# Moving the bias of an attention's softmax to ScalarE and fusing VectorE's three passes into one

## The chip, the cores and the metric

The kernel runs on one core of a Trainium2 chip. The metric is the device time of one execution in microseconds (us). The engines named here are TensorE (PE; its weight loads are shown apart, as PEld), VectorE (DVE), ScalarE (ACT), GpSimd (POOL) and SyncE (SP), which only issues transfers. Each engine takes its instructions strictly in the order of its own queue: an instruction that waits holds up all that stand behind it on that engine, and nothing else.

## The reference

A small transformer in float32 with T = 1024 tokens and C = 512 features: x = x + attention_a(LN(x)), then a feed-forward part, x = x + attention_b(LN(x)), and a second feed-forward part with the same weights. The change concerns attention_b alone, the second attention: 32 heads of 128 features in 8 groups of 4, one k and v per group, q and k normalised by the root of their mean square, and a bias that grows with the distance of two tokens.

```python
q = _rmsnorm(q, q_norm_w)
k = _rmsnorm(k, k_norm_w)
...
scores = jnp.einsum('bkgqd,bksd->bkgqs', qg, k) / math.sqrt(HD)
rel = pos[None, :] - pos[:, None]
bias = jnp.where(rel > 0, NEG_INF, slopes[:, :, None, None] * rel)
attn = jax.nn.softmax(scores + bias[None], axis=-1)
out = jnp.einsum('bkgqs,bksd->bkgqd', attn, v)
...
return out @ Wo.T
```

`rel` is never positive where a score counts (the mask is causal), and `slopes` has one number per head.

## The kernel before

Tokens are worked in 8 tiles of 128 (`NT`). For a query tile i only the keys of tiles 0 to i count, so a tile's row of scores is w = (i + 1) x 128 wide, 128 to 1024 columns, and is made in chunks of up to 512 columns (`QC`). The second attention is `attention_b`, L722 to L1151, some 475 to 1530 us of the profiled execution.

For each group g:

- `project_kv` (L810) makes k and v for 8 tiles on PE (L825). ACT sums k's squares (`ksq`, L833) and copies k and v out of PSUM (L835, L836); POOL scales k by its norm; k is transposed into `kT` (L862).
- `project_q` (L866) makes q for the 4 heads, each in two halves of 512 tokens (pq_h_0, pq_h_1; L878). The results lie in `ps_m`, a PSUM pool of two buffers. Of each half ACT writes the squares (`qsq`, L891), and after it VectorE the weighted q (`qT`, L893); then the buffer is free.
- `sum_squares` (L899) sums a head's squares on PE (st, L910), also in a buffer of `ps_m`; VectorE transposes the sums (`by`, L916), which frees the buffer, scales and shifts them (L920), and POOL raises them to the power -1/2 (`rsqrt`, L97, the instruction is L103). So `rq` holds, for each token, the reciprocal norm of q divided by the head's slope. It is needed by that head's softmax, later on.
- `softmax(g, hh, i)` (L923) does one tile of one head. PE makes the scores of a chunk (L932) into `ps_s`, again two buffers; VectorE writes p = s * rq + rel (L934), from PSUM into the tile's buffer p in SBUF. The mask lies in `rel` as a huge negative number. When the row is whole, VectorE takes its negated maximum (`nm`, L938) and multiplies it by the slope (L939); ACT computes exp(slope * p + nm) in place and sums the row (L941); VectorE takes the reciprocal (L943); POOL scales the row (L944). The pool `pp` has four buffers p (L760).
- `columns` (L957) turns p on VectorE in blocks of 32 x 32 (`pT` for the first four key tiles, L959; `tT` for the rest, L965). After the last of these p is free. `product` multiplies with v (L993), and ACT copies the result out (L1026).
- `project_o` (L737) multiplies with Wo (L742), and VectorE adds to x (L748).

A tile's `columns` come two tiles after its softmax (`LAG`, L1048). The main loop (L1087 to L1136) runs heads 0 to 3 of a group and tiles 7 down to 0. Between the softmaxes it spreads other matmuls as filler, so that PE has work while the softmax goes through VectorE and ACT: the next group's `project_kv`, then the output projection of the group before, then the next group's `project_q`. The shares are in `SHARE` (L1062). The last head of the last group runs its tiles upward.

The order of each engine's queue is decided by a scheduler when the kernel is built, from dependencies and priorities, so an edit in one place can move instructions elsewhere. A name such as s_3_6_0 is the score chunk of head 3, tile 6, from column 0; y_2 belongs to head 2. For odd tiles the rows are rotated by 32-row blocks, and `rels` holds `rel` and its rotated copy `relr`.

A fused pass of the kind that the change uses is there already: the first attention (L357) adds a mask to scores in PSUM and reduces them in the same instruction, with a constant scale and a mask in bf16.

Of the kernel before, what the change touches and what calls it, by code (L numbers as in the profile page):

```python
# [9 lines left out]
F32 = mybir.dt.float32  # L10
BF16 = mybir.dt.bfloat16
AF = mybir.ActivationFunctionType
ALU = mybir.AluOpType
AX = mybir.AxisListType
PSUM = bass.MemoryType.PSUM

P = 128
T = 1024
NT = T // P
# [6 lines left out]
NEG = -(2.0**100)  # L26
# [10 lines left out]
GRP = HB // HKV  # L37
DB = 128
B = 32
RMS_EPS = 1e-6  # L40
# [8 lines left out]
def alibi_slopes(n_heads):  # L49
    start = 2 ** (-(2 ** (-(math.log2(n_heads) - 3))))  # L50
    return [start * start**i for i in range(n_heads)]
# [13 lines left out]
class Block:  # L65
# [656 lines left out]
    def attention_b(self, ctx, wo_pool, WqT, WkT, WvT, WoT, qw, kw, xnT, missing, ffn_weights):  # L722
# [4 lines left out]
        nc, tc, sm = self.nc, self.tc, self.sm  # L727
        slopes = alibi_slopes(HB)
# [28 lines left out]
        with ExitStack() as ctx:  # L757
# [31 lines left out]
            rels = [self.rel, cp.tile([P, T], F32, tag="relr", name="relr")]  # L789
# [9 lines left out]
            kTs, vs, qTs, rqs = {}, {}, {}, {}  # L799
# [50 lines left out]
            def by_tile(t, i0, i1, turn=-1):  # L850


                v = t[:, i0 * P : i1 * P].rearrange("p (i a c) -> p a i c", a=P // B, c=B)
                return v[:, :, i0 % 2 :: 2], v[:, ::turn, 1 - i0 % 2 :: 2]
# [3 lines left out]
            def k_columns(g, half, k_sb, kT):  # L858

                pool, tag = (ps_m, "m") if g else (ps_s, "s")  # L860
                ps = self.transpose4(pool, [k_sb[:, a, :] for a in range(4)], f"k{g}{half}", tag=tag)
                nc.scalar.activation(  # L862
                    kT[:, half * QC : (half + 1) * QC], ps.rearrange("p a b -> p (a b)"), AF.Copy, scale=kw_sb
                )

            def project_q(g, wq):  # L866

                qTs[g] = []
                rqs[g] = []
                for hh in range(GRP):  # L870
                    qT = qp.tile([P, T], F32, tag="qT", name=f"qT{g}_{hh}")
                    qTs[g].append(qT)
                    rqs[g].append(sm.tile([P, NT], F32, tag="rq", name=f"rq{g}_{hh}", bufs=6))
                    for qc in range(NQC):
                        cols = slice(qc * QC, (qc + 1) * QC)
                        ps = ps_m.tile([P, QC], F32, tag="m", name=f"pq{g}_{hh}_{qc}")
                        for kc in range(KC):
                            nc.tensor.matmul(  # L878
                                ps, lhsT=wq[:, kc, hh * DB : (hh + 1) * DB], rhs=xnT[:, kc, cols], start=(kc == 0), stop=(kc == KC - 1)
                            )  # L880
                            if kc < KC - 1:
                                yield
                            if kc == 2 and qc == 0 and squares:

                                sum_squares(*squares.pop(0))
                            if kc == 1 and g and later:
                                k_columns(*later.pop(0))
                        if qc == 0:
                            sq = work.tile([P, T], F32, tag="w", name=f"qsq{g}_{hh}", bufs=1)
                        for to, of in zip(by_tile(sq, qc * 4, qc * 4 + 4), by_tile(ps, 0, 4, 1)):  # L890
                            nc.scalar.activation(to, of, AF.Square)  # L891
                        for to, of in zip(by_tile(qT, qc * 4, qc * 4 + 4), by_tile(ps, 0, 4, 1)):
                            nc.vector.tensor_scalar_mul(to, of, qw_sb)  # L893
                        yield
                        if later and not g:
                            k_columns(*later.pop(0))
                    squares.append((g, hh, sq))

            def sum_squares(g, hh, sq_T, behind=False):  # L899

                rq = rqs[g][hh]
                st = ps_m.tile([P, QC], F32, tag="m", name=f"st{g}_{hh}")[:, : NT * B]
                for a, sq in enumerate(sq_T.rearrange("p (i a c) -> a p i c", a=P // B, c=B)):
                    with ExitStack() as ctx:
                        if behind:
                            ctx.enter_context(tc.high_priority(offset=2000))
                        ins = nc.tensor.matmul(  # L910
                            st[a * B : (a + 1) * B, :].rearrange("p (i c) -> p i c", c=B), lhsT=ones, rhs=sq, start=True, stop=True
                        )
                        if behind:
                            tc.keep_in_program_order(ins)
                by_token = work.tile([P, NT, B], F32, tag="st", name=f"by{g}_{hh}", bufs=1)
                nc.vector.transpose(by_token.rearrange("p i c -> p (i c)"), st)  # L916


                s2 = slopes[g * GRP + hh] ** 2
                nc.vector.tensor_scalar(rq, by_token[:, :, 0], s2, DB * RMS_EPS * s2, ALU.mult, ALU.add)  # L920
                self.rsqrt(rq, rq, [NT])

            def softmax(g, hh, i):  # L923
                slope = slopes[g * GRP + hh]
                qT, kT, rq = qTs[g][hh], kTs[g], rqs[g][hh]
                w = (i + 1) * P
                n = f"{g}_{hh}_{i}"
                p = pp.tile([P, T], F32, tag="p", name=f"p{n}")
                for lo in range(0, w, QC):
                    hi = min(lo + QC, w)  # L930
                    s = ps_s.tile([P, QC], F32, tag="s", name=f"s{n}_{lo}")[:, : hi - lo]
                    nc.tensor.matmul(s, lhsT=qT[:, i * P : (i + 1) * P], rhs=kT[:, lo:hi], start=True, stop=True)  # L932
                    at = (NT - 1 - i) * P
                    nc.vector.scalar_tensor_tensor(  # L934
                        p[:, lo:hi], s, rq[:, i : i + 1], rels[i % 2][:, at + lo : at + hi], ALU.mult, ALU.add
                    )
                nm = sm.tile([P, 1], F32, tag="nm", name=f"nm{n}")
                nc.vector.tensor_reduce(nm, p[:, :w], AX.X, ALU.max, negate=True)  # L938
                nc.vector.tensor_scalar_mul(nm, nm, slope)  # L939
                ss = sm.tile([P, 1], F32, tag="ss", name=f"ss{n}")  # L940
                nc.scalar.activation(p[:, :w], p[:, :w], AF.Exp, bias=nm, scale=slope, accum_out=ss)  # L941
                rs = sm.tile([P, 1], F32, tag="rs", name=f"rs{n}")
                nc.vector.reciprocal(rs, ss)  # L943
                nc.gpsimd.tensor_scalar(p[:, :w], p[:, :w], rs, 1.0, ALU.mult, ALU.mult)  # L944
                return p
# [104 lines left out]
            for n, _ in enumerate(in_turn(project_kv(0, wkv), project_q(0, wq))):  # L1050
                missing(n, ps_s, "s")
# [12 lines left out]
            def finish(g, hh, i, p):  # L1064
                while rest:
                    product_rest(*rest.pop(0))
                columns(hh, p, i)
                last = g == HKV - 1
                if last and hh == GRP - 1:

                    if i == NT // 2 - 1:
                        product(g, hh, 0, NT // 2)
                    elif i == NT - 1:
                        product(g, hh, NT // 2, NT, whole=True)
                elif i == 0:
                    product(g, hh, 0, NT, whole=last and hh > 1)
                    while squares:
                        sum_squares(*squares.pop(0), behind=True)
                    if hh == GRP - 1:
                        while kept:  # L1080
                            copies(*kept.pop(0))
                    if last and hh == 1:
                        product_rest(g, heads[:2])
                    elif not last and hh == GRP - 1:
                        rest.append((g, heads))

            for g in range(HKV):  # L1087
# [4 lines left out]
                if not last:  # L1092
                    wq, wkv = load_qkv(g + 1)
                    parts.append(project_kv(g + 1, wkv))
                    parts.append(project_q(g + 1, wq))
# [8 lines left out]
                for hh in range(GRP):  # L1104
# [8 lines left out]
                    for at, i in enumerate(range(NT) if last and hh == GRP - 1 else down):  # L1113
                        p = softmax(g, hh, i)
                        n = hh * NT + at + 1
# [189 lines left out]
```

## Time and profile before

| what | value |
|---|---|
| median of 3 runs | 1589.62 us (1589.33 to 1589.82) |
| profiled execution, span | 1587.1 us |
| PE busy | 1576.2 us |
| DVE busy | 1084.9 us |
| ACT busy | 569.7 us |
| POOL busy | 364.4 us |
| granted PE clock | 1.00 throughout |

The profiled execution's own time is known by its span, 1587.1 us, from its first to its last instruction; the median of the runs lies 2.5 us above it. A group line of the profile reads: line of the code, engine, operation, output <- inputs, shapes and count, then the busy time of all and the mean duration of one in ns, then the time that the engine was idle just before them and what ended it. A line of waits reads: engine and instruction, what it waited for, us in total, how many times, the longest. A line of a timeline reads: start in us, duration in us, engine, line, operation, output <- inputs, count of records. A float32 matmul leaves two records.

### The profile page before, as it was taken

The numbers are of one execution on the slowest core, as the hardware profiler recorded it, in microseconds if no ns is written. First come the engines' busy times: TensorE is split into PE (matmuls) and PEld (weight loads), VectorE is DVE, ScalarE is ACT, GpSimd is POOL, SyncE is SP. The second block draws the span as 40 slices with busy tenths as digits, with TensorE's granted clock in tenths as the row PEclk, the third lists the DMA queues.
The fourth block names the chain that finished last, engine by engine and source line by source line (L and its number), as shares of the span: only waits on it lengthen the run. The fifth ranks groups of instructions, "written<-read, shape, count | busy, mean of one in ns | idle before, by whom it ended". The sixth has DMA issues, their size and how long they took to land.

```text
span 1587.1 us, 31573 instructions
## 1 busy us (share of the span) xinstructions
PE 1576.2 (99%) x12574; PEld 934.3 (59%) x12574; DVE 1084.9 (68%) x2841; ACT 569.7 (36%) x1397; POOL 364.4 (23%) x480
## 2 busy tenths in 40 slices
PE   9999999999999999999999999999999999999999
PEld 5545555555566557657556655756665566566654
DVE  4558788773535895775786678587667757777753
ACT  2216666664223443233233223323423322322330
POOL 3000000002222333222223213222322222222350
PEclk9999999999999999999999999999999999999999
DMA  5000332222022002002100200200110020010001
GB/s 206 1 1 6 24 20 18 20 19 63 1 72 70 20 27 68 27 1 55 40 27 28 68 27 1 73 22 28 45 49 27 27 74 28 1 54 28 2 2 53
DMA packets 66419, 56.42 MB, mean 36 GB/s; under 512 B 9504, under 2 KB 51232, under 8 KB 66272
## 3 DMA queue, kind: packets, MB, share of 16 engines
q1 hardware_dynamic: 64960, 50.46, 13.7%
q0 software_dynamic: 784, 2.90, 0.5%
q8 instruction: 99, 1.62, 0.4%
q10 hardware_dynamic: 528, 1.05, 0.2%
q14 instruction: 48, 0.39, 0.1%
HBM read 30.98 MB, written 2.10 MB: 21 GB/s over the span
## 4 chain that ended last, share of the span: by engine, by line
PE 95%; DVE 2%; POOL 1%; ACT 1%; issue 0%; DVEq 0%; ACTq 0%; POOLq 0%
PE s L932 15%; PE pq L878 14%; PE wo L742 13%; PE o L993 11%; PE sT L386 8%; PE kv L825 6%; PE oT L428 5%; PE or L993 4%; PE pm_f L693 3%; PE s L337 3%; PE pj_v L197 2%; PE pj_q L197 2%; PE pm_ao L1185 2%; PE pj_k L197 2%; PE st L910 1%; PE sT L406 1%
## 5 line engine op out<-in xcount | busy, mean ns | idle before, releaser
L941 ACT ACTIVATE p<-p,nm 128x1024 f32<-128x1024 f32 (+7 forms) x256 | 198.1, 774 | 379.9 <-DVE nm L939 362.0
L944 POOL TENSOR_SCALAR p<-p,rs 128x1024 f32<-128x1024 f32 (+7 forms) x256 | 191.0, 748 | 583.7 <-DVE rs L943 563.8
L932 PE MATMUL s<-kT,qT 128*128 128x512 f32 (+3 forms) x768 | 294.7, 492 | 0.7 <-DVE p L934 0.5
L878 PE MATMUL pq<-xnTb,wq 128*128 128x512 f32 x512 | 241.0, 596 | 0.0
L932 PEld LDWEIGHTS s<-kT,qT 128*128 128x128 f32 x768 | 141.4, 190 | 168.8 <-issue 111.4
L742 PE MATMUL wo<-wo,oT 128*128 128x512 f32 x512 | 239.7, 593 | 0.8 <-ACT spare L750 0.8
L959 DVE STREAM_TRANSPOSE pT<-p 128x512 f32<-128x512 f32 (+3 forms) x256 | 152.9, 603 | 80.3 <-PE o L993 47.4
L938 DVE TENSOR_REDUCE nm<-p 128x1 f32<-128x1024 f32 (+7 forms) x256 | 188.0, 735 | 2.8
L993 PEld LDWEIGHTS o<-pT,va 32*128 32x128 f32 x4212 | 174.4, 185 | 22.4 <-issue 11.5
L408 ACT ACTIVATE p<-sT 128x512 f32<-128x512 f32 (+1 forms) x292 | 155.2, 592 | 90.0 <-PE s L337 35.1
L993 PE MATMUL o<-pT,va 32*128 32x224 f32 (+5 forms) x4212 | 181.3, 324 | 0.0
L337 PE MATMUL s<-kT,qT 32*128 32x512 f32 (+3 forms) x768 | 164.5, 520 | 0.0
L386 PE MATMUL sT<-qT,kT 32*128 32x128 f32 (+3 forms) x1152 | 155.5, 402 | 0.4 <-ACT p L408 0.4
L742 PEld LDWEIGHTS wo<-wo,oT 128*128 128x128 f32 x512 | 94.7, 190 | 89.2 <-issue 77.2
L878 PEld LDWEIGHTS pq<-xnTb,wq 128*128 128x128 f32 x512 | 92.9, 190 | 90.0 <-issue 77.9
L934 DVE SCALAR_TENSOR_TENSOR p<-s,rq,relr 128x512 f32<-128x512 f32 x192 | 121.0, 644 | 11.3 <-PE s L932 11.2
L825 PE MATMUL kv<-wkv,xnTb 128*128 128x256 f32 x512 | 118.2, 381 | 0.2
L965 DVE STREAM_TRANSPOSE tT<-p 128x512 f32<-128x512 f32 (+3 forms) x128 | 63.9, 499 | 74.8 <-PE or L993 45.9
L934 DVE SCALAR_TENSOR_TENSOR p<-s,rq,rel 128x512 f32<-128x512 f32 (+1 forms) x192 | 103.5, 560 | 11.9 <-PE s L932 10.9
L386 PEld LDWEIGHTS sT<-qT,kT 32*128 32x128 f32 x1152 | 80.7, 184 | 50.7 <-issue 28.6
L825 PEld LDWEIGHTS kv<-wkv,xnTb 128*128 128x128 f32 x512 | 95.1, 190 | 20.9 <-issue 3.4
L354 DVE TENSOR_REDUCE part<-s 128x1 f32<-128x512 f32 x128 | 81.5, 684 | 28.2 <-PE s L337 20.1
(156 smaller groups left out, 1716.6 us busy)
## 6 DMA issues: line engine op xcount, KB each, us to landing
va<-v SPq DMA_DIRECT2D x256, 64.0 KB
wq<-in_b_WqT_dram SPq DMA_DIRECT2D x8, 1024.0 KB
wo<-in_b_WoT_dram SPq DMA_DIRECT2D x8, 1024.0 KB
x<-in_x_dram SPq DMA_DIRECT2D x8, 256.0 KB
wkv<-in_b_WkT_dram SPq DMA_DIRECT2D x8, 256.0 KB
wkv<-in_b_WvT_dram SPq DMA_DIRECT2D x8, 256.0 KB
out_dram<-x SPq DMA_DIRECT2D x7, 256.0 KB
o<-oTs SPq DMA_DIRECT2D x48, 32.0 KB
```

What stands on the lines that cost most here:

```text
L337: nc.tensor.matmul(made[j][:, at:end], lhsT=qT[rows_of(j), c, i * P : (i + 1) * P], rhs=kT[rows_of(j), c, kc * QC : kc * QC + end - at], s ...
L386: nc.tensor.matmul(made[j][:, at:end], lhsT=kT[rows_of(j), c, b * P : (b + 1) * P], rhs=qT[rows_of(j), c, qc * QC + x0 : qc * QC + x1], st ...
L408: nc.scalar.activation(p[:, j, :end], made[j][:, :end], AF.Exp)
L742: nc.tensor.matmul(ps, lhsT=oTs[g, h][:, t * P : (t + 1) * P], rhs=wo[:, h, :], start=(h == heads[0]), stop=(h == heads[-1]))
L825: nc.tensor.matmul(ps.rearrange("p a b -> p (a b)"), lhsT=xnT[:, kc, i * P : (i + 1) * P], rhs=wkv[:, kc].rearrange("p a b -> p (a b)"), s ...
L878: nc.tensor.matmul(ps, lhsT=wq[:, kc, hh * DB : (hh + 1) * DB], rhs=xnT[:, kc, cols], start=(kc == 0), stop=(kc == KC - 1))
L932: nc.tensor.matmul(s, lhsT=qT[:, i * P : (i + 1) * P], rhs=kT[:, lo:hi], start=True, stop=True)
L934: nc.vector.scalar_tensor_tensor(p[:, lo:hi], s, rq[:, i : i + 1], rels[i % 2][:, at + lo : at + hi], ALU.mult, ALU.add)
L938: nc.vector.tensor_reduce(nm, p[:, :w], AX.X, ALU.max, negate=True)
L941: nc.scalar.activation(p[:, :w], p[:, :w], AF.Exp, bias=nm, scale=slope, accum_out=ss)
L944: nc.gpsimd.tensor_scalar(p[:, :w], p[:, :w], rs, 1.0, ALU.mult, ALU.mult)
L993: nc.tensor.matmul(cols(o[:, a], j, j + skip), lhsT=vs[g][j // 4][rows, j % 4 * NB + b, :], rhs=moving(j, j + skip, rows, slice(b * B, (b ...
```

## The change

With y = (sum of squares) + 128 eps, the old kernel keeps rq = 1 / (slope * sqrt(y)) and computes s * rq + rel, of which softmax takes slope times. The new one keeps -1 / sqrt(y) in `rq`, and a second column `irq` = slope * sqrt(y), made on VectorE as y * slope * y^(-1/2). Now

- ACT writes rel * irq (128 x w, one factor per row) into the tile's buffer p before the scores come (new activation with Copy);
- VectorE adds the scores to it, multiplies by -1 / sqrt(y) and takes the running minimum, in one `tensor_tensor_reduce` per chunk; the minimum of the first chunk is the start of the second;
- ACT's Exp takes this minimum as its bias and -1 as its scale.

The separate reduce and the multiplication of its result by the slope are gone. In `sum_squares` VectorE has two more small instructions per head: `irq`, which reads POOL's power, and the negation of `rq`. The pool for `rq` gets a second tag for `irq`; `nm` has 6 buffers. Nothing changes on PE, POOL and the transfers but the order in which the scheduler puts a few of them.

```diff
-                    rqs[g].append(sm.tile([P, NT], F32, tag="rq", name=f"rq{g}_{hh}", bufs=6))
+                    rqs[g].append([sm.tile([P, NT], F32, tag=t, name=f"{t}{g}_{hh}", bufs=6) for t in ("rq", "irq")])
...
-                s2 = slopes[g * GRP + hh] ** 2
-                nc.vector.tensor_scalar(rq, by_token[:, :, 0], s2, DB * RMS_EPS * s2, ALU.mult, ALU.add)
-                self.rsqrt(rq, rq, [NT])
+                y = sm.tile([P, NT], F32, tag="y", name=f"y{g}_{hh}")
+                nc.vector.tensor_scalar_add(y, by_token[:, :, 0], DB * RMS_EPS)
+                self.rsqrt(rq, y, [NT])
+
+                nc.vector.scalar_tensor_tensor(irq, y, slopes[g * GRP + hh], rq, ALU.mult, ALU.mult)
+                nc.vector.tensor_scalar_mul(rq, rq, -1.0)
...
+                at = (NT - 1 - i) * P
+
+                nc.scalar.activation(p[:, :w], rels[i % 2][:, at : at + w], AF.Copy, scale=irq[:, i : i + 1])
+                nm = -NEG
                 for lo in range(0, w, QC):
...
-                    at = (NT - 1 - i) * P
-                    nc.vector.scalar_tensor_tensor(
-                        p[:, lo:hi], s, rq[:, i : i + 1], rels[i % 2][:, at + lo : at + hi], ALU.mult, ALU.add
-                    )
-                nm = sm.tile([P, 1], F32, tag="nm", name=f"nm{n}")
-                nc.vector.tensor_reduce(nm, p[:, :w], AX.X, ALU.max, negate=True)
-                nc.vector.tensor_scalar_mul(nm, nm, slope)
+                    least = sm.tile([P, 1], F32, tag="nm", name=f"nm{n}_{lo}", bufs=6)
+                    nc.vector.tensor_tensor_reduce(
+                        out=p[:, lo:hi],
+                        in0=s,
+                        in1=p[:, lo:hi],
+                        scale=rq[:, i : i + 1],
+                        scalar=nm,
+                        op0=ALU.add,
+                        op1=ALU.min,
+                        accum_out=least,
+                    )
+                    nm = least
                 ss = sm.tile([P, 1], F32, tag="ss", name=f"ss{n}")
-                nc.scalar.activation(p[:, :w], p[:, :w], AF.Exp, bias=nm, scale=slope, accum_out=ss)
+                nc.scalar.activation(p[:, :w], p[:, :w], AF.Exp, bias=nm, scale=-1.0, accum_out=ss)
```

In the changed kernel the new instructions are at L920 (y), L921 (power), L923 (irq), L924 (negation), L933 (bias copy), L940 (fused pass) and L952 (Exp).

More of the change, by code (lines that the diff above doesn't have):

```diff
@@ L899, in sum_squares @@
             def sum_squares(g, hh, sq_T, behind=False):
-                rq = rqs[g][hh]
+                rq, irq = rqs[g][hh]
                 st = ps_m.tile([P, QC], F32, tag="m", name=f"st{g}_{hh}")[:, : NT * B]
@@ L916, in sum_squares @@
                 nc.vector.transpose(by_token.rearrange("p i c -> p (i c)"), st)
-                s2 = slopes[g * GRP + hh] ** 2
-                nc.vector.tensor_scalar(rq, by_token[:, :, 0], s2, DB * RMS_EPS * s2, ALU.mult, ALU.add)
-                self.rsqrt(rq, rq, [NT])
+                y = sm.tile([P, NT], F32, tag="y", name=f"y{g}_{hh}")
[3 more added lines that the diff above has]
+                nc.vector.tensor_scalar_mul(rq, rq, -1.0)
             def softmax(g, hh, i):
-                slope = slopes[g * GRP + hh]
-                qT, kT, rq = qTs[g][hh], kTs[g], rqs[g][hh]
+                qT, kT, (rq, irq) = qTs[g][hh], kTs[g], rqs[g][hh]
                 w = (i + 1) * P
```

## The prediction

> **What bounds the kernel now.** I read first the page's busy shares and its chain of work, then stretches of the second attention one by one, then the groups of instructions by form, then the waits, and last the timeline of one place.
>
> ```profile
> span 1587.1 us, 31573 instructions
> PE 1576.2 (99%) x12574; PEld 934.3 (59%) x12574; DVE 1084.9 (68%) x2841; ACT 569.7 (36%) x1397; POOL 364.4 (23%) x480
> ...
> PE 95%; DVE 2%; POOL 1%; ACT 1%; issue 0%; DVEq 0%; ACTq 0%; POOLq 0%
> ```
>
> TensorE (PE) is the bound: 95% of the chain. A busy share is an average, so here are two stretches of the second attention (about 475 to 1530 us), and the sum over 500 to 1500 us. The columns are PE, PEld, DVE, ACT and POOL busy, then the granted clock.
>
> ```profile
> 600.00:700.00 100.00, 99.97 (x724) 60.77 (x720) 71.01 (x173) 29.23 (x78) 25.12 (x36) 1.00 0.14 38
> 900.00:1000.00 100.00, 100.00 (x632) 56.91 (x631) 78.79 (x195) 33.40 (x87) 25.35 (x31) 1.00 0.09 29
> sum 1000.00, PE 999.22 PEld 615.96 DVE 733.81 ACT 328.37 POOL 273.88; mean PE 99.92 PEld 61.60 DVE 73.38 ACT 32.84 POOL 27.39
> ```
>
> In the whole stage PE is idle for 0.8 us, at a clock of 1.00. Busy time can hide slack, so I also compared starts: a record of 512 columns is followed by the next after 429 ns where nothing disturbs, 384 after 322, 256 after 215. From 490 to 1500 us all matmuls together start only 15 us later than this, 122 times by about 104 ns. So work taken off VectorE (DVE) can bring little, while a wait that reaches PE costs its full length. The question is what the change does to in-order queues, not to sums.
>
> The rows that price the change (line, engine, operation, count | busy us, mean ns | idle before):
>
> ```profile
> L938 DVE TENSOR_REDUCE nm<-p 128x1 f32<-128x1024 f32 (+7 forms) x256 | 188.0, 735 | 2.8
> ...
> L939 DVE TENSOR_SCALAR nm<-nm 128x1 f32<-128x1 f32 x256 | 35.3, 138 | 2.6
> L357 DVE CUSTOM_DVE_ANT_0 junk<-s,mask,part 128x512 f32<-128x512 f32 x32 | 22.1, 729 | 6.4 <-PE s L337 6.4
> L357 DVE DVE_READ_ACCUMULATOR2_ANT neg<- 128x1 f32 x256 | 21.0, 82 | 0.0
> ...
> L941 ACT ACTIVATE p<-p,nm 128x1024 f32<-128x1024 f32 (+7 forms) x256 | 198.1, 774 | 379.9 <-DVE nm L939 362.0
> ...
> L103 POOL TENSOR_TENSOR rq<-rq,mhalf 128x8 f32<-128x8 f32 x32 | 52.6, 1645 | 90.7 <-DVE rq L920 90.0
> ```
>
> The last one matters most: the power of -1/2 on GpSimd (POOL) takes 1645 ns. Before, no VectorE instruction waits for it except, much later, the scores of that head.
>
> **The change part by part.**
>
> *Removed from DVE*: 256 reduces, 188.0 us, and 256 small scalings, 35.3 us.
>
> *Replaced on DVE*: 384 scalar-tensor-tensor passes (L934, 730 to 738 ns at 512 columns, 224.5 us in all) become 384 fused passes, each of two instructions. Its nearest row is the first attention's fused pass, the same call with a PSUM source: 729 ns at 512 columns, and 82 ns for reading the accumulator; its second source is bf16, here f32. From below 688 + 82 (the row without a running scalar); from above 730 + 672, the old pass and the 512-column reduce. I take 729 + 82 as the closest row: about +31 us for 384. Together DVE loses some 180 us (with the additions below), 68% to 57% of the span. Hidden under PE either way: worth nothing by itself.
>
> [...]
>
> *Added on ACT*: 256 bias copies (128 x w, a scale per row). Priced by the Exp rows without their accumulator read, 198.1 us (128 columns 399, 1024 columns 1148); from below by 186 (the scaled copy into kT takes 688 at 512 columns where Exp takes 721), from above by 198.1 + 48.1, if a read as after each Exp came along. ACT goes from 36% to 48%. By load it is hidden; but ACT's queue is in order, and Exps and the squares of q (`qsq`, L891) now stand behind copies that wait for a free buffer among four, or for `irq`.
>
> *Added on DVE, 32 times*: `irq` (0.2 us, priced by L920's 201) and the negation (0.15, by L939), 11 us. `irq` waits for the POOL power. In the changed kernel's order it stands right behind y or one chunk later, so DVE stands about 1.6 us at it, 32 times. Behind it wait fused passes (which free the two score buffers), the q evictions `qT` and the transposes `by` (which free the two buffers of `ps_m`). PE waits for those. Price: from below nothing, where PE holds enough queued work; from above 1.65 us x 32 = 53 us by itself.
>
> *The order.* Some other DVE instructions move too. The place I work out is the end of head 2's q projection, before it (matmul, then VectorE):
>
> ```profile
> 851.55 0.64 PE L910 MATMUL st<-qsq,ones 128*32 128x256 f32 x8
> 852.12 1.98 PE L878 MATMUL pq<-xnTb,wq 128*128 128x512 f32 x4
> ```
>
> ```profile
> 849.18 0.85 DVE L893 TENSOR_SCALAR qT<-pq,qw_sb 128x256 f32<-128x256 f32 x2
> ...
> 852.26 0.45 DVE L916 STREAM_TRANSPOSE by<-st 128x256 f32<-128x256 f32 x1
> ...
> 853.57 0.71 DVE L959 STREAM_TRANSPOSE pT<-p 128x512 f32<-128x512 f32 x1
> ```
>
> The sums st are done at 852.12, `by` frees their buffer by 852.71, and pq_3_1 (head 3, second half), which needs that buffer, is due at 852.98. In the changed order `by` stands behind the transposes pT of tiles 4 and 3 of the running head and the pass of tile 2; pq_3_1 is due at 852.98 + 0.43 = 853.41, as scores of 256 columns come first. The chain by rows, with 0.05 to 0.1 us per handover: the sums before end 839.75, their `by` (431), pT of tile 6 (701) and y_1 (201) 841.1; power to 842.85; irq_1 843.05; second pass of tile 5 (480 + 82) 843.65; its Exp (931 + 188) 844.85, on ACT ahead of qsq (2 halves, 0.66) 845.5; qT 846.4; pass of tile 4, 847.2; pT of tile 5 (0.70) 847.9; second chunk of tile 4 (346 + 82, overlapped) 848.25; its Exp (826 + 188) 849.3; qsq 849.95; qT 850.85; pass of tile 3 (811) 851.65; pT and tT of tile 4, 852.55; meanwhile Exp of tile 3 (721 + 188) 852.6; reciprocal 852.8; POOL (695) 853.55; pT of tile 3, 854.3; pass of tile 2 (613 + 82) 855.0; `by` (431) 855.4. That is 2.0 us after pq_3_1 is due; with the delays carried into it I had 2.25.
>
> In the same way, for one group: pq_1_1 waits 1.7 us for `by` of head 0 (behind the pass of tile 1, pT of tile 2 and their POOL multiply); the first scores of tile 6 of head 3 wait 0.6, of tile 3 0.25, of the next head's tile 7 0.1; kv_1 of the next group waits 0.6 for qT of pq_3_1 (now behind the last pT; before, qT ends 860.45 and kv_1 starts in time at 860.61); kv_2 0.35 for ACT. Heads 0 and 1, where the filler is the output projection and no irq falls, keep 0.35 to 0.7 us of slack: nothing. Sum 5.85 per group, six full preparations: 35; the first group some 4; the start of the stage 1.4 (ACT's four first copies, 3.9 us, wait for irq_0 ahead of qsq of pq_1_1, so the next sums' buffer comes late): 40.
>
> Places under 0.5 us are below what such chains resolve, and the first group was worked out least. I take the four larger: 1.7 + 0.6 + 2.25 + 0.6 = 5.15, x 6 = 30.9, + 1.4 = 32 us. Nothing is deducted for the tail (at 1511 to 1516 us PE waits 1.0 us for ACT and 0.8 us for a transpose), since ACT is busier there and DVE less.
>
> The profiled execution's span is 1587.1; the median of the runs is 1589.62, 2.5 us more, taken as unchanged. Forecast 1589.6 + 32 = about 1621 us, +2.0%.
>
> **The rivals.**
>
> *Hidden (1589, within 0.2%).* For it: DVE and ACT keep over 40% idle, each tile loses a reduce (0.28 to 1.20 us) and a scaling before its Exp, which shortens the chain as much as irq lengthens it, and sums and `by` are seldom urgent. Against it: before, `by` meets its deadline at the place above by 0.27 us only. Its price is 0 to 3 us.
>
> *Faster (about 1585).* 40 of the 104-ns delays lie between two score matmuls; if all are late passes on DVE and go, 4.2 us, with 1 us of the tail. More than the 15 us of all excess starts can't be had in this stage, so 1575 is the floor. Against it: the same delays occur between q-projection matmuls of one buffer, where DVE has no part. It decides only if the irq waits never reach PE.
>
> *Slower by far (about 1655).* The fused pass costs its upper bound, 730 + 672 at 512 columns, 0.59 us more than I took. The passes cover 32 heads x 4608 = 147,456 columns, so 170 us come back to DVE; DVE is then as busy as before but with longer single steps, and each maximum is up to 1.2 us later. If a fifth of it reaches PE, as through the same buffers, 34 us come on top of the 32. It decides from about 1.0 us per pass, where the fused pass costs more than the row of the reduce gave back. For it: 362 us of ACT's idle time are waits for nm, so every Exp follows its maximum closely. Against it: the row with a PSUM source and a running scalar shows no such cost.
>
> **How the numbers follow.** A measurement of this kernel tells about 0.2% from no change. Slower as worked out (1595 to 1640): 0.60; slower by far: 0.16; hidden: 0.13; faster: 0.09; the rest, 0.02, is a gain beyond the tail's. Slower by over 0.2% is 0.60 + 0.16 and a part of hidden, 0.77; same 0.13 less that part, 0.12; faster 0.11. The range goes down to 1587, leaving out faster, and up to 1655, leaving out half of slower by far. The likeliest case's own range is from one place per group at its bare slack (1.2 us x 6, 1597) to all 40 us and a quarter more, 1640.
>
> **What would show it.** Right: DVE waits for POOL at irq, some 30 times, 40 us or more; PE waits in the preparing stretches (pq for `by`, scores for the pass, kv for qT), none while the output projection fills; DVE near 905 us, ACT near 768, clock 1.00. Wrong: PE still above 99.5% in 500 to 1500 us (hidden); the fused pass far from 811 at 512 columns with its read; waits of PE spread evenly over all heads (ACT as a second clock).

## The result and the profile after

The changed kernel takes 1616.75 us (median of 4 runs, 1615.92 to 1616.95) against 1589.57 us: ratio 1.017, 95% interval 1.0155 to 1.0184. The profiled execution's span is 1615.0 us, 27.9 us above that of before. The page of the changed kernel, its span, busy shares, chain and two of its groups:

```profile
span 1615.0 us, 32171 instructions
...
PE 1585.9 (98%) x12574; PEld 931.5 (58%) x12574; DVE 917.6 (57%) x2777; ACT 744.8 (46%) x1653; POOL 364.8 (23%) x480
...
PE 75%; DVE 11%; POOL 6%; ACT 4%; issue 3%; SPq 1%; DMA 0%; POOLq 0%; DVEq 0%; ACTq 0%
...
L938 PE MATMUL s<-kT,qT 128*128 128x512 f32 (+3 forms) x768 | 296.9, 495 | 6.5 <-DVE nm L940 6.4
...
L878 PE MATMUL pq<-xnTb,wq 128*128 128x512 f32 x512 | 242.9, 599 | 8.1 <-DVE by L916 8.1
```

VectorE lost 167 us of work, ScalarE gained 175, and PE, which does the same 12574 matmuls at the same clock, 1.00, now stands: the chain runs through PE for 75% of the span instead of 95%. Most of the rest, 21%, goes through the loop VectorE, POOL, ScalarE. The idle time in the last column is what PE waits, and for whom.

Busy time by stretch, the same two as before and the sum over 500 to 1500 us (columns PE, PEld, DVE, ACT, POOL):

```profile
600.00:700.00 100.00, 99.23 (x733) 62.16 (x732) 52.23 (x156) 45.10 (x109) 24.70 (x35) 1.00 0.14 38
900.00:1000.00 100.00, 98.95 (x620) 54.62 (x620) 60.97 (x182) 48.48 (x102) 25.12 (x33) 1.00 0.09 27
sum 1000.00, PE 985.20 PEld 598.41 DVE 557.87 ACT 484.71 POOL 262.80; mean PE 98.52 PEld 59.84 DVE 55.79 ACT 48.47 POOL 26.28
```

PE stands 14.8 us in these 1000 us, where it stood 0.8, and of the other engines none is above 56% in the sum. No engine took PE's place as the bound; PE waits for the length of chains.

Comparing the starts of successive matmuls with the dense spacing, as in the prediction, accounts for the whole difference. The table sums how much later than this spacing the matmuls start, its excess, from 470 us on, in us:

| kernel | up to group 2's k and v | six groups | last group and after | sum |
|---|---|---|---|---|
| before | 3.0 | 10.4 | 7.0 | 20.5 |
| changed | 7.8 | 29.7 | 11.4 | 48.9 |

The sums differ by 28.4, the spans by 27.9. The six groups (1 to 6, in which the k, v and q of groups 2 to 7 are made) lose 3.2 us each, two thirds of it at the same three places each time: 0.94 us ahead of pq_1_1, 0.74 ahead of pq_3_1 and 0.45 ahead of the first scores of head 3's tile 6. The remainder, about 1.1 us a group, comes in small pieces: 0.15 to 0.2 us at k and v (0.5 to 0.6 at kv_1 in two of the groups), partly there before, and more of the 104-ns delays.

What PE waits for between 600 and 1420 us, by the view of waits (us in total, times, longest):

```profile
PE pq L878 <- DVE by L916: 8.1, 12, 0.8
PE s L938 <- DVE nm L940: 2.0, 7, 0.3
PE kv L825 <- DVE qT L893: 0.3, 1, 0.3
```

Twelve waits for `by`, two for each of six groups. And VectorE's new wait, from the same view over the whole run:

```profile
DVE irq L923 <- POOL rq L103: 44.2, 32, 1.8
```

The place that the prediction worked out in group 2, here at the end of group 1 of the changed kernel (timeline, VectorE, then PE):

```profile
724.84 0.71 DVE L970 STREAM_TRANSPOSE pT<-p 128x512 f32<-128x512 f32 x1 [0.89 <-POOL p L955]
725.48 0.58 DVE L940 CUSTOM_DVE_ANT_0 p<-s,p,rq 128x384 f32<-128x384 f32 x1
...
725.98 0.45 DVE L916 STREAM_TRANSPOSE by<-st 128x256 f32<-128x256 f32 x1
...
728.39 0.17 DVE L923 SCALAR_TENSOR_TENSOR irq<-y,rq 128x8 f32<-128x8 f32 x1 [1.76 <-POOL rq L103]
```

```profile
723.77 0.64 PE L910 MATMUL st<-qsq,ones 128*32 128x256 f32 x8
...
726.48 1.98 PE L878 MATMUL pq<-xnTb,wq 128*128 128x512 f32 x4 [0.58 <-DVE by L916]
```

The sums are done at about 724.4. `by` could start then, but ahead of it in VectorE's queue stands pT of tile 3, which waits 0.89 us for POOL's multiply, and then the pass of tile 2. So `by` ends at 726.43 and pq_3_1 starts at 726.48. The irq wait of 1.76 us comes after `by` and isn't itself ahead of pq_3_1; the one of the head before, 13 us earlier, is in the chain: without it, in the first run below, this place doesn't wait.

### The profile page after: what moved, and what is told of

Read it like the earlier page. It is cut to its first block, busy times and chain, and to the rows that moved or that the text cites. A ratio compares the mean times of both kernels' runs of the same rounds, so it can differ in the third digit from the quotient of the medians.

```text
span 1615.0 us, 32171 instructions
## 1 busy us (share of the span) xinstructions
PE 1585.9 (98%) x12574; PEld 931.5 (58%) x12574; DVE 917.6 (57%) x2777; ACT 744.8 (46%) x1653; POOL 364.8 (23%) x480
## 4 chain that ended last, share of the span: by engine, by line
PE 75%; DVE 11%; POOL 6%; ACT 4%; issue 3%; SPq 1%; DMA 0%; POOLq 0%; DVEq 0%; ACTq 0%
PE o L1004 12%; PE wo L742 11%; PE s L938 9%; PE sT L386 8%; PE kv L825 6%; PE oT L428 5%; DVE p L940 4%; PE pm_f L693 3%; PE or L1004 3%; DVE pT L970 3%; PE pq L878 3%; PE s L337 3%; POOL p L955 2%; ACT p L952 2%; POOL rq L103 2%
## 5 line engine op out<-in xcount | busy, mean ns | idle before, releaser
L952 ACT ACTIVATE p<-p,nm 128x1024 f32<-128x1024 f32 (+7 forms) x256 | 197.1, 770 | 210.7 <-DVE nm L940 197.2
L940 DVE CUSTOM_DVE_ANT_0 p<-s,p,rq 128x512 f32<-128x512 f32 (+3 forms) x256 | 159.9, 626 | 17.8 <-PE s L938 16.9
L933 ACT ACTIVATE p<-relr,irq 128x1024 f32<-128x1024 f32 (+3 forms) x128 | 106.1, 829 | 115.1 <-DVE tT L976 67.7
L933 ACT ACTIVATE p<-rel,irq 128x896 f32<-128x896 f32 (+3 forms) x128 | 92.0, 719 | 50.8 <-DVE pT L970 28.2
L954 DVE RECIPROCAL rs<-ss 128x1 f32<-128x1 f32 x256 | 40.3, 157 | 124.1 <-ACT p L952 123.2
```

What stands on the lines that cost most here:

```text
L933: nc.scalar.activation(p[:, :w], rels[i % 2][:, at : at + w], AF.Copy, scale=irq[:, i : i + 1])
L940: nc.vector.tensor_tensor_reduce(out=p[:, lo:hi], in0=s, in1=p[:, lo:hi], scale=rq[:, i : i + 1], scalar=nm, op0=ALU.add, op1=ALU.min, acc ...
```

## The experiments

Three causes were possible, and the prediction had mixed them: (1) VectorE stands at irq; (2) `by` stands behind transposes that wait for Exp, reciprocal and POOL, an order that comes with the shorter fused pass; (3) the bias copies hold up ScalarE's queue. The first four runs take away or add one at a time.

**irq on POOL**, so that VectorE never waits for the power:

```diff
-                nc.vector.scalar_tensor_tensor(irq, y, slopes[g * GRP + hh], rq, ALU.mult, ALU.mult)
-                nc.vector.tensor_scalar_mul(rq, rq, -1.0)
+                nc.gpsimd.tensor_scalar(irq, y, slopes[g * GRP + hh], 1.0, ALU.mult, ALU.mult)
+                nc.gpsimd.tensor_tensor(irq, irq, rq, ALU.mult)
+                nc.gpsimd.tensor_scalar(rq, rq, -1.0, 1.0, ALU.mult, ALU.mult)
```

> The changed kernel, with irq and the negation of rq computed on POOL behind the power (three small POOL instructions per head), so that no VectorE instruction waits for the power. All of the computation is kept. Theory 1 (VectorE standing at irq is what reaches PE): the 44.2 us of waits at irq go, and most of the 27 us with them: 1589 to 1598 us. Theory 2 (the transposes `by` stand behind pT, which wait for the chain Exp, reciprocal, POOL, and this order comes with the shorter fused pass): the places pq_1_1 and pq_3_1 keep their 0.9 and 0.7 us per group; some 1606 to 1617 us. Theory 3 (ACT's queue with the copies holds up Exp and qsq): at most 5 us less, 1611 to 1617 us.

Measured 1607.72 us, 9.0 less than the changed kernel. The time lies in theory 2's range, but only one of its two places is left, so no theory has it alone. The waits of PE from 600 to 1400 us tell which place went:

```profile
PE pq L878 <- DVE by L916: 4.5, 6, 0.8
PE s L939 <- DVE nm L941: 3.5, 6, 0.6
```

Six waits for `by` are left of twelve: those of pq_1_1 (0.92 us each in the spacing). Those of pq_3_1 are gone, while the first scores of head 3's tile 6 now wait 0.76 instead of 0.45 us. So irq is in the chain of the one place and not in that of the other.

**No bias copy**: the fused pass adds rel unscaled.

```diff
-                nc.scalar.activation(p[:, :w], rels[i % 2][:, at : at + w], AF.Copy, scale=irq[:, i : i + 1])
...
-                        in1=p[:, lo:hi],
+                        in1=rels[i % 2][:, at + lo : at + hi],
```

> The changed kernel without ACT's bias copies: the fused pass adds rel itself, not rel * irq, so the bias isn't scaled by the row norm (the output is not the reference's). irq is still computed on VectorE and waited for, but read by nobody. Theory 3 (copies): ACT falls to about 550 us busy, and most of the 27 us go: 1589 to 1598 us. Theory 1 (irq): little changes, 1608 to 1617 us. Theory 2 (order of `by`): the two places of `by` stay, 1603 to 1613 us.

Measured 1608.17 us, 8.6 less, inside the ranges of theories 1 and 2, with ScalarE back at 567.5 us busy. Both waits for `by` stay (0.71 and 0.78 us a group); the wait of head 3's tile 6 for its scores' buffer is gone in the repeating groups. The copies cost a part, again no more than a third.

**The kernel before with the irq wait added**:

```diff
                 self.rsqrt(rq, rq, [NT])
+                irq = sm.tile([P, NT], F32, tag="irq", name=f"irq{g}_{hh}", bufs=6)
+                nc.vector.scalar_tensor_tensor(irq, rq, slopes[g * GRP + hh], rq, ALU.mult, ALU.mult)
+                nc.vector.tensor_scalar_mul(irq, irq, -1.0)
```

> The kernel before, with two added VectorE instructions per head behind the power (128x8, one waits for POOL, the second is a negation); nobody reads them. The computation is the kernel before's. Theory 1: VectorE stands about 1.5 us, 32 times, and with its higher load PE loses 10 to 30 us: 1600 to 1620 us. Theories 2 and 3: 1589 to 1594 us.

Measured 1602.54 us, 13.1 more than before (ratio 1.0082, 1.0067 to 1.0097): the wait alone, with the order that comes with it, costs half of what the whole change costs. VectorE's wait in the whole run, then PE's from 600 to 1400 us:

```profile
DVE irq L923 <- POOL rq L103: 36.3, 32, 1.8
```

```profile
PE kv L825 <- ACT v L836: 5.1, 6, 0.9
```

It reaches PE at another place than in the changed kernel. One such place in its timeline, VectorE, ScalarE and PE:

```profile
882.89 0.17 DVE L923 SCALAR_TENSOR_TENSOR irq<-rq 128x8 f32<-128x8 f32 x1 [1.11 <-POOL rq L103]
...
884.48 0.15 DVE L942 TENSOR_SCALAR nm<-nm 128x1 f32<-128x1 f32 x1
```

```profile
884.73 0.93 ACT L944 ACTIVATE p<-p,nm 128x768 f32<-128x768 f32 x1 [0.72 <-DVE nm L942]
...
885.66 0.24 ACT L835 COPY k<-kv 128x128 f32<-128x128 f32 x1
885.81 0.27 ACT L836 COPY v<-kv 128x128 f32<-128x128 f32 x1
```

```profile
886.12 1.99 PE L825 MATMUL kv<-wkv,xnTb 128*128 128x256 f32 x8 [0.86 <-ACT v L836]
```

irq stands between the two chunks of tile 5; its maximum comes late, ScalarE waits for it, and behind that Exp stand the copies of k and v that free PE's buffer. Between VectorE's wait and PE's there are two more in-order queues.

**The kernel before with the bias copies added** (written into the buffer, then overwritten):

```diff
+                at = (NT - 1 - i) * P
+                nc.scalar.activation(p[:, :w], rels[i % 2][:, at : at + w], AF.Copy, scale=rq[:, i : i + 1])
```

> The kernel before, with ACT's 256 bias copies added (rel times rq, written into the tile's buffer before the scores and then overwritten by the scalar-tensor-tensor pass). The result is the kernel before's. ACT grows by about 198 us. Theory 3: copies wait for buffers and hold up Exp and qsq, PE loses 10 us or more: 1600 us and above. Theories 1 and 2: 1589 to 1594 us.

Measured 1591.68 us, ratio 1.0014 (1.0005 to 1.0024), with ScalarE at 747.0 us busy. So 177 us more on ScalarE cost about 2 us by themselves. By itself theory 3 is a small cause here; why the copies cost 8.6 in the changed kernel, this run doesn't tell.

The next four runs take both away, move `by` forward, or do both.

**Neither**: no irq, no copy, the negation on POOL. What is left is the fused pass.

> The changed kernel with neither: irq is left out, the negation of rq is on POOL, and the fused pass adds rel itself, so the bias isn't scaled by the row norm (the output is not the reference's). What is left of the change is the fused pass and the order that comes with it. If the three causes add: 1616.7 - 9.0 (irq) - 8.6 (copies), about 1599 us, with the wait of pq_1_1 for `by` still about 0.9 us per group. If irq and copies are the whole cause and hid behind each other: 1588 to 1592 us.

Measured 1598.66 us: the losses add, as the 1599 had it, though pq_1_1 waits 0.71 us a group by the spacing and not 0.9. The fused pass, with the order that comes with it, relieves VectorE of 170 us, adds no work to ScalarE and still costs 9 us (ratio 1.0056, 1.0041 to 1.0071). PE waits, whole run (those of the second line lie outside 600 to 1400 us):

```profile
PE pq L878 <- DVE by L916: 3.3, 6, 0.6
PE s L936 <- DVE nm L938: 2.6, 4, 1.4
```

**Neither, and the sums one matmul earlier**:

```diff
-                            if kc == 2 and qc == 0 and squares:
+                            if kc == 1 and qc == 0 and squares:
```

In VectorE's queue `by` of head 0 then stands ahead of pT of tile 2 and the pass of tile 1, and `by` of head 2 ahead of pT of tile 3 and the pass of tile 2.

> As the run `neither` (bias not scaled by the row norm, irq left out), and the sums of squares st one matmul earlier in the q projection, which puts `by` ahead of the transposes of tile 2 in VectorE's order. If the order of `by` is the third cause: back to 1588 to 1593 us, no wait of pq_1_1 and pq_3_1 for `by`. If it isn't: as `neither` or slower, since st now needs its buffer 0.86 us sooner.

Measured 1592.36 us, 6.3 less than `neither` and 2.8 above the kernel before, and no wait of pq for `by` from 600 to 1400 us; in its place

```profile
PE st L910 <- DVE qT L893: 1.3, 6, 0.2
```

**irq on POOL, and the sums earlier**, complete in its computation:

> The run `irq_on_pool` with the sums st one matmul earlier; all of the computation is kept. If the order of `by` is the third cause, the 0.93 us per group at pq_1_1 go, and a part of the start's loss: 1597 to 1602 us. If st's earlier need of a buffer costs as much, no change, 1606 to 1610 us.

Measured 1596.24 us, 11.5 less than with irq on POOL alone.

**The changed kernel, and only the sums earlier**:

> The changed kernel, complete, with only the sums st one matmul earlier. If the order of `by` is a cause by itself: 5 x (0.94 + 0.74) = 8 us less in the steady groups, some 1606 to 1610 us. If irq stands behind both places: 1613 us or more, as irq then stands earlier before the passes of tiles 2 and 1.

Measured 1602.49 us, 14.3 less than the changed kernel, more than either side expected. One moved line takes back half the loss. By the spacing both waits for `by` are gone in all six groups (the expectation had counted five), and so is the wait of tile 6's scores, which it hadn't counted; VectorE stands 36.9 us at irq instead of 44.2. An early `by` also brings y, the power and irq forward, which would explain the last two; it wasn't tested apart. From here irq on POOL is worth another 6.3, and leaving out irq and the copies altogether 3.9 more.

**Control: the kernel before with the sums earlier.**

> The kernel before, with only the sums st one matmul earlier; the computation is unchanged. A control for the runs with early sums. If the earlier place only mends what the changed kernel's order broke, nothing moves here: 1588 to 1591 us. If st waits for its buffer, some 0.4 us per group, 1591 to 1594 us.

Measured 1589.93 us, ratio 1.0002 (0.9993 to 1.0011). The earlier place mends nothing there, since in the old order `by` followed its sums at once (0.07 us after them at the two places, at 824.14 and 852.26).

**The rest.** By the spacing, irq on POOL with early sums has 11.2 us of excess in the six groups (before: 10.4), but 6.7 against 3.0 up to group 2 and 10.4 against 7.0 at the end. So the first and the last group were put back to the old form:

```diff
+            OLD = (0, HKV - 1)
...
+                if g in OLD:
+                    s2 = slopes[g * GRP + hh] ** 2
+                    nc.vector.tensor_scalar(rq, by_token[:, :, 0], s2, DB * RMS_EPS * s2, ALU.mult, ALU.add)
+                    self.rsqrt(rq, rq, [NT])
+                    return
...
+                if g in OLD:
...
+                        nc.vector.scalar_tensor_tensor(
+                            p[:, lo:hi], s, rq[:, i : i + 1], rels[i % 2][:, at + lo : at + hi], ALU.mult, ALU.add
+                        )
...
+                    nc.vector.tensor_reduce(nm, p[:, :w], AX.X, ALU.max, negate=True)
+                    nc.vector.tensor_scalar_mul(nm, nm, slope)
```

> The run `irq_on_pool_sums_early`, with the first and the last group in the old form (three passes, no bias copy, no irq) and the six groups between in the new; all of the computation is kept. If what is left of the loss (6.7 us) lies in the first and last group, as the spacing of the matmuls has it (3.8 and 3.4 us, 0.6 in the six groups between): 1589 to 1592 us. If it moves with the new form: 1594 to 1597 us. A gain over the kernel before would need fewer of the 104-ns delays, at most 2 us.

Measured 1590.32 us, ratio 1.0005 (0.9996 to 1.0014): the rest did lie there. With irq off VectorE's queue, the sums early and the old form at both ends, the new form costs nothing that can be measured; it also gains nothing, with VectorE at 950.6 us instead of 1084.9. No version beat the kernel before.

## Why the prediction was right

Forecast 1621 and +2.0%, measured 1616.75 and +1.7%. The mechanism held: VectorE's relief bought nothing, waits at irq (44.2 us, 32 times; "40 us or more") and late `by` reached PE through the two buffers of `ps_m`, in the preparing stretches of each group, at the same clock of 1.00.

*Terms that held.* VectorE ended at 917.6 us busy, where about 905 was forecast. The bias copies, 198.1 us forecast: 106.1 and 92.0 in the two groups of rows. ScalarE's busy time grew by less, 175, to 744.8 and not near 768, since instructions that follow directly overlap (a copy from 732.33 for 0.93 us, the next from 733.16). irq and the negation: 167 and 185 ns.

*Terms that were mis-sized.* The fused pass, 31 us more than the old: 44 (268.8 with its reads, against 224.5). The forms show where it comes from; p is the tile's buffer, nm the running minimum, and L357 the first attention's pass without a running value:

```profile
L940 DVE CUSTOM_DVE_ANT_0 p<-s,p,rq 128x512 f32<-128x512 f32 x160 | 116.4, 728 | 17.6 <-PE s L938 16.7
L940 DVE DVE_READ_ACCUMULATOR2_ANT nm<- 128x1 f32 x384 | 31.8, 83 | 0.0
L940 DVE CUSTOM_DVE_ANT_0 p<-s,p,nm 128x512 f32<-128x512 f32 x32 | 25.9, 809 | 4.1
...
L357 DVE CUSTOM_DVE_ANT_0 junk<-s,mask 128x512 f32<-128x512 f32 x32 | 20.8, 689 | 5.3 <-PE s L337 4.9 <-PE sT L386 0.3
...
L940 DVE CUSTOM_DVE_ANT_0 p<-s,p,rq 128x128 f32<-128x128 f32 x32 | 10.7, 334 | 0.0
L357 DVE CUSTOM_DVE_ANT_0 junk<-s,mask 128x128 f32<-128x128 f32 x32 | 9.1, 285 | 0.0
```

First chunks take 728, as forecast, but partly by luck: the row of 729 carries a running value, which a first chunk doesn't (it reads the factor rq for each row instead, where the first attention's scale is constant); the row without a running value, 688 before, was the forecast's lower bound. Second chunks, with a minimum carried in, take 809. VectorE has room for the 13 us; what they add to a chain that reaches PE, no run shows apart.

*The chain to pq_3_1*, 2.0 to 2.25 us forecast, 0.74 measured, is the step that was furthest off. Counted from the end of head 2's product (839.18 there, 711.41 in the trace after), the chain had irq_1 done at 3.87 us (3.74 measured), qT of pq_2_0 at 7.2 (6.8), qT of pq_2_1 at 11.7 (10.8), pT of tile 3 at 15.1 (14.1) and `by` at 16.2 (15.0); pq_3_1 was due at 14.2 (14.3). Every instruction is there, in this order, and the sum is too long by some 0.06 us a step: I added a duration and a handover, while on one engine a following instruction starts before the one ahead is recorded as done (the pass at 718.15 lasts 0.74, yet pT starts at 718.82, with the accumulator's read at the same moment). Some twenty steps make 1.2 us, more than half of the wait. pq_1_1 was forecast too long as well, 1.7 against 0.94, and the scores of tile 6, 0.6 against 0.45; kv_1's 0.6 was 0.2 in four of the groups and 0.5 to 0.6 in two. These chains aren't gone through here.

*Terms that were left out.* The six groups lost 19.3 us, not 30.9. What made the total come out close are two omissions: the start of the stage and the first group lost 4.8 (1.4 taken, the 4 us for the first group dropped as least worked out), and the end 4.4, for which nothing was put. In the end PE waits for the last tiles, for instance

```profile
1539.43 2.83 PE L1004 MATMUL o<-pT,va 32*128 32x128 f32 x90 [1.37 <-DVE pT L970]
```

The closeness of 1621 is therefore part mechanism, part luck of errors of opposite sign: 11.6 us too much in the groups, 7.8 too little at the two ends.

*What the prediction had wrong about cause.* It worked the new place of `by` into its chains, but took irq as what makes them late. No cost of its own stood in the sum for the order without irq, and for the copies only the 1.4 us at the start. The runs give irq 9.0, the copies 8.6 and the fused pass with its order 9.1 us, and moving only the sums and their `by` forward takes back 14.3. That all three matter follows from the runs; why the scheduler put `by` behind pT was not tried.

*The rivals.* Hidden, faster: excluded by the ratio's interval. Slower by far hung on a fused pass of about 1.0 us or more at 512 columns; it took 0.73 to 0.81, and 0.08 for its read. Its f32 second source brought no such price: from 128 to 512 columns the pass of a first chunk grows from 334 to 728 ns, the first attention's with its bf16 mask and without a running value from 285 to 689, that is 394 and 404 ns for 384 columns; with a value carried in they grow from 390 to 809 and from 346 to 728, 419 and 382.

## What to carry to other kernels

Where one engine is dense, as PE here, load taken off the others can be worth nothing (167 us less on VectorE saved no time here), and each instruction that waits on another engine is to be judged by what stands behind it in its queue, two queues further if need be (at one place of the kernel before with the wait added, 1.11 us at irq reached PE as 0.86). A shorter pass can also cost time, 9 us here: the order of the queues is made anew, and something that freed a buffer at once may end up behind something that waits; look up in the new order what stands ahead of each instruction that frees a scarce buffer. When chains of rows are added, subtract the overlap of neighbours (some 0.06 us a step here), and price the first and last round of a loop apart (4.8 and 4.4 us here).

## What the runs showed that was not expected

In a first chunk the fused pass takes no more time per column with its f32 second source than the first attention's with bf16 (394 and 404 ns for 384 columns; 419 and 382 with a value carried in). A carried-in minimum costs it 81 ns more at 512 columns (809 against 728), a carried-in value costs the first attention's pass 39 (728 against 689). And the same 175 to 180 us of ScalarE don't have one price: the copies cost 2.3 us in the kernel before, 8.6 in the changed kernel, and at most 3.9 where irq had been moved to POOL and `by` forward. That this depends on what else is late fits these runs, but isn't shown.
